# First tile's query products in another order, with VectorE's readings and a set of weight sums in other places

## The chip, the cores and the metric

The kernel runs on one core of a Trainium2 chip. A core has TensorE (matrix products, called PE in the profile), VectorE (DVE), ScalarE (ACT), GpSimd (POOL) and SyncE (SP), which issues most of the transfers here. Each engine works through its own list of instructions in the order in which they were written, and waits on semaphores for the others. The metric is the device time of one execution in microseconds (us); smaller is better.

## The reference

One layer of attention with many query heads and one shared key and value head, for 64 batches of 128 tokens with 512 features. Cut to what matters:

```python
xn = layernorm(x, g_in)                        # x: (64, 128, 512)
q = (xn @ Wq).reshape(b, n, 16, 64) * 64**-0.5 # Wq: (512, 1024)
k, v = split(xn @ Wkv)                         # Wkv: (512, 128)
k, v = [null_key; k], [null_value; v]          # null_kv: 2 rows of cond_64
sim = q @ k.T + [null_attn_bias; attn_bias]    # attn_bias: (16, 128, 128)
sim = -max where the key lies ahead of the query or is masked
out = softmax(sim) @ v                         # (64, 16, 128, 64)
out = out.reshape(b, n, 1024) @ Wo             # Wo: (1024, 512)
return x + layernorm(out, g_out)
```

All of it is float32.

## The kernel before

Four batches form a *group* (16 groups), two batches a *pair* (32 pairs). The main loop goes over pairs, `for d in range(1, 30): turn(d); body(d)`, and ends with two pairs of shorter work. While the softmax of pair d runs, a body also makes half of the queries, keys and values of the next group, and projects the output of pair d - 1 through Wo. So three pairs are in flight, and TensorE always has products of some stage to do. The order of every engine's work is the order of the calls in the source: there is no scheduler that changes it.

*`turn(d)`* makes the scores of the pair's two batches a and b, adds them to the bias (`scores_add`, VectorE), takes maxima, and multiplies the previous pair's weights by the values (`values`, L805). The sums with the bias free the PSUM tiles into which `values` then writes.

*`body(d)`* is what the change touches. With h = d % 2 it handles two tiles of queries, f0 = 2h and f1 = 2h + 1. Bodies with even d are called even, the others odd. A query tile is not made by eight products of blocks but by seven, with sums of blocks of weights (`wS`) and of tokens (`xS`, made by `token_sum` on GpSimd), as in Winograd's form of Strassen's method. `product(g, f, k, ...)` (L539) is product k, two matmuls of 128x256 in the source, four in the trace (the float32 passes are seen apart). They add up in two PSUM tiles:

- `pa` holds product 1; a copy `p1` (L551, ScalarE) is kept. Product 6 is added to it, and a copy `u2` is kept. Product 7 is added, and a copy `u3` is kept. Product 4 is added, and the tile is copied out (L557).
- `pc` holds product 5; with `u3` it gives one part of the result (`q_out`, L560, VectorE). Product 3 is added; with `u2` it gives another (L560 again). Only then may the next tile's product 5 take `pc`.

Each addition into `pa` must wait until ScalarE has made the copy before it; product 3 must wait for the first reading of `pc`.

Product 2 gives the last part. From d = 2 on (`deep`) it is itself made of seven small products for two tiles at once (`inner_product`, L605, tile `pl`), whose results are read by `inner_out` (L621, VectorE). Their weight sums are made once, by `weight_sums_inner` (L578, VectorE), in body 1, which still makes product 2 whole. Their token sums are made in each even body by `token_sums_inner` (L584, GpSimd).

The output projection is made in the same way: `out_sum` (L872, GpSimd), `out_product` (L892), copies `out_keep` (L906), readings `out_part` (L922, VectorE).

Around these a body carries: the exponentials (`exps`, L707, ScalarE), their reciprocal (`rinv`, L725, VectorE) and the scaling by it (`scale`, L729, GpSimd); `blocks_T` (L745, VectorE); the norm of a finished pair's output, namely `pair_norm` (L950, ScalarE), `pair_gain` (L953, VectorE), `pair_residual` (L956, VectorE) and the store; and the norm of the input of a later group, `norm_stats` (VectorE, with a power on GpSimd at L280), `norm_apply` (L301, ScalarE) and the transposes `tokens_T` (L325, VectorE). The last of these are done where `xw` is true, which it is not in the last two bodies (d = 28 and 29). `bias_add` (L641, GpSimd) lays out the bias of a later batch.

Of the kernel before, what the change touches and what calls it, by code (L numbers as in the profile page):

```python
# [17 lines left out]
def kernel(  # L18
# [66 lines left out]
    HC = NC // 2  # L85
# [423 lines left out]
    def token_sum(g, k):  # L509

        xS[g, k] = gp.tile([P, GB // 2, HK, N], FP, tag=f"xS{k}", name=f"xS{k}_{g}", bufs=1)
        lo, hi = xT[g][:, 0 : GB // 2], xT[g][:, GB // 2 :]
        b11, b12 = lo[:, :, lo_k], hi[:, :, lo_k]
        b21, b22 = lo[:, :, hi_k], hi[:, :, hi_k]
        p, m = {
            1: (b12, b11),
            2: (b22, xS.get((g, 1))),
            3: (b22, b12),
            4: (b21, xS.get((g, 2))),
        }[k]  # L520
        nc.gpsimd.tensor_tensor(xS[g, k], p, m, ALU.subtract)
# [58 lines left out]
    def token_sums_inner(g):  # L580

        x = gp.tile([P, 4, N], FP, tag="xL", name=f"xL_{g}", bufs=1)
        lo = xT[g][:, 0 : GB // 2]
        nc.gpsimd.tensor_tensor(x[:, 0:2], lo[:, 1, hi_k], lo[:, :, HK], ALU.subtract)  # L584
        nc.gpsimd.tensor_tensor(x[:, 2], lo[:, 1, KC - 1], x[:, 0], ALU.subtract)
        nc.gpsimd.tensor_tensor(x[:, 3], lo[:, 0, KC - 1], x[:, 2], ALU.subtract)
        xL[g] = x
# [114 lines left out]
    def exps(b, hf, lo=0, hi=R8):  # L702
        if hf == 0 and lo == 0:
            rsum[b] = small.tile([P, 2, R8], FP, tag="rsum", name=f"rsum_{b}")
        for k in range(lo, hi):
            row = S[b][:, k, WITH_NULL[hf]]
            nc.scalar.activation(  # L707
                row,
                row,
                AF.Exp,  # L710
                bias=nmax[b][:, hf, k : k + 1],
                accum_out=rsum[b][:, hf, k : k + 1],
            )
# [555 lines left out]
    def body(d):  # L1269

        a, b, p, l = 2 * d, 2 * d + 1, 2 * d - 2, 2 * d - 4
        g, h = d // 2 + 1, d % 2
        q, soft = g < NG, d > 0
        out, ln = 0 <= p <= P_LAST, 0 <= l <= P_LAST
        xw = g + 1 < NG
        m = (g + 1) * GB + 2 * h
        sums = q and h == 0 and d > 0
        f0, f1 = 2 * h, 2 * h + 1
        deep = q and d > 1

        if q:
            tags = [q_tags[g - 1, f, h] for f in range(NF)]
            q_tiles(g, (f0, f1), tags)
            pkv = kv_pair(g * GB + 2 * h)
        if soft:
            scores_max(b, 0)
            rinv(a, 0)
            scale(a, 0)
        if ln:
            pair_stats(l + 1)  # L1290
            pair_pow(l + 1)
        if sums:
            token_sums_inner(g)
        if q:
            kv_pair_out(g * GB + 2 * h, pkv)
            if h == 1:
                keys_T(g)
                values_spread(g)
        if h == 0 and g + 1 < NG:
            load_mask(g + 1)  # L1300
        if ln:
            pair_nmr(l)
            pair_nmr(l + 1)
        if xw:
            norm_stats(m)
            norm_stats(m + 1)
        if soft:
            scores_max(a, 1)
        if q:
            product(g, f0, 1, ps_q, "a")  # L1310
            keep("a", "p1")
        if ln:
            pair_norm(l)
        if deep:
            inner_product(g, h, 1)
            inner_out(g, h, 0, 0, 0, "p1")
        elif q:
            product(g, f0, 2, ps_w, "w")
            q_out(g, f0, 0, "w", "p1")
        if soft:  # L1320
            scores_max(b, 1)
        if xw:
            norm_nmr(m)
            norm_nmr(m + 1)
        if ln:
            pair_gain(l)
            pair_residual(l)
            store(l)
        if soft:
            exps(b, 0, 0, 4)  # L1330
        if sums:
            token_sum(g, 3)
        if out:
            out_sum(p, 0)
        if sums:
            token_sum(g, 4)
        if out:
            out_product(p, 1, ps_y, "X")
            out_keep("X", "yp1", "yp1")
            out_sum(p, 1)  # L1340
            out_sum(p, 2)
        if soft:
            exps(b, 0, 4, 6)
        if ln:
            pair_norm(l + 1, (ps_y, "Y"))
        if q:
            product(g, f0, 5, ps_q, "c")
            product(g, f0, 6, ps_q, "a", start=False)
            keep("a", "u2")
        if soft:  # L1350
            exps(b, 0, 6)
            rinv(b, 0)
        if out:
            out_product(p, 2, ps_w, "w")
            out_part(p, 0, "w", "yp1")
            out_sum(p, 3)
        if soft:
            scale(b, 0)
        if xw:
            norm_apply(m)  # L1360
        if q:
            product(g, f0, 7, ps_q, "a", start=False)
            keep("a", "u3")
        if deep:
            for k in (6, 5, 2):
                inner_product(g, h, k)
            inner_out(g, h, 0, 1, 0, "p1")
        if q:
            q_out(g, HC + f0, 1, "c", "u3")
        if deep:  # L1370
            inner_out(g, h, 0, 0, 2)
        if ln:
            pair_gain(l + 1)
            pair_residual(l + 1)
            store(l + 1)
        if xw:
            norm_apply(m + 1)
            tokens_T(m)
        if soft:
            exps(a, 1, 0, 1)  # L1380
        if q and not deep:
            product(g, f1, 2, ps_w, "w")
        if q:
            product(g, f0, 4, ps_q, "a", start=False)
            q_out(g, HC + f0, 0, "a")
            product(g, f0, 3, ps_q, "c", start=False)
            q_out(g, f0, 1, "c", "u2")
        if xw:
            tokens_T(m + 1)
            if h == 1:  # L1390
                tokens_out(g + 1)
                tokens_in(g + 1)
        if 0 <= p:
            for r in (p, p + 1):
                load_res(r)
        nm = m + 2
        if nm < B and xw:
            load_x(nm)
            load_x(nm + 1)
        if soft:  # L1400
            exps(a, 1, 1, 4)
        if q:
            product(g, f1, 1, ps_q, "a")
            keep("a", "p1")
        if deep:
            inner_product(g, h, 7)
            inner_out(g, h, 1, 1, 0, "p1")
            inner_out(g, h, 1, 1, 1)
        elif q:
            q_out(g, f1, 0, "w", "p1")  # L1410
        if soft:
            exps(a, 1, 4)
            rinv(a, 1)
            scale(a, 1)
            exps(b, 1, 0, 2)
        if q:
            product(g, f1, 5, ps_q, "c")
        if out:
            out_product(p, 5, ps_y, "Y")
            out_keep("Y", "yp5", "yp5")  # L1420
        if soft:
            exps(b, 1, 2, 3)
        if q:
            product(g, f1, 6, ps_q, "a", start=False)
            keep("a", "u2")
        if deep:
            inner_product(g, h, 4)
            inner_product(g, h, 3)
            inner_out(g, h, 1, 0, 0, "p1")
            inner_out(g, h, 0, 1, 1)  # L1430
        if soft:
            exps(b, 1, 3)
            blocks_T(a)
        if out:
            out_product(p, 6, ps_y, "X", start=False)
            out_keep("X", "yu2", "yu2")
        if soft:
            rinv(b, 1)
            scale(b, 1)
        if q:  # L1440
            product(g, f1, 7, ps_q, "a", start=False)
            keep("a", "u3")
            q_out(g, HC + f1, 1, "c", "u3")
        bias_add(b + 2)
        if d == PAIRS - 3:
            bias_add(B - 1)
        if out:
            out_product(p, 3, ps_y, "Y", start=False)
            out_part(p, 1, "Y", "yu2")
        if q:  # L1450
            product(g, f1, 3, ps_q, "c", start=False)
            q_out(g, f1, 1, "c", "u2")
        if out:
            pair_stats(p)
            pair_pow(p)
            out_product(p, 7, ps_y, "X", start=False)
            out_part(p + 1, 1, "X", "yp5")
        if soft:
            blocks_T(b)
        if q:  # L1460
            product(g, f1, 4, ps_q, "a", start=False)
            q_out(g, HC + f1, 0, "a")
        if out:
            out_product(p, 4, ps_y, "X", start=False)
            out_part(p + 1, 0, "X")
        if d == 1:
            weight_sums_inner()

    def gains_T():
        pg = ps_y.tile([P, KC], FP, tag="X", name="pg")  # L1470
# [177 lines left out]
```

## Time and profile before

| what | value |
|---|---|
| median of 3 runs | 1052.17 us (1051.85 to 1052.64) |
| profiled execution, its own time | 1051.84 us |
| its span, first to last instruction | 1050.0 us |
| granted TensorE clock, mean | 0.996 |
| TensorE busy | 1029.7 us (98%) |
| VectorE busy | 795.2 us (76%) |
| GpSimd busy | 745.5 us (71%) |
| ScalarE busy | 678.2 us (65%) |
| DMA, all queues | 105.13 MB, mean 100 GB/s |

The span leaves out what lies around the instructions, here 1.84 us. A row of the timeline reads: start in us, duration in us, engine, source line, operation, the tiles written and read, their shapes, how many instructions were merged, and in brackets the idle time before it and who ended it. A row of the waits reads: engine, its tile and line, for whom it waited, then microseconds in total, times, and the longest. A row of a window reads: stretch, its length, then for TensorE, its weight loads, VectorE, ScalarE and GpSimd the busy time and the number of instructions, then the granted clock, the DMA share and GB/s. Matmuls are pipelined, and their ends are modelled; so starts are compared with starts.

### The profile page before, as it was taken

What the parts mean: (1) busy time and instruction counts of PE and PEld (TensorE: products, weight loads), DVE (VectorE), ACT (ScalarE), POOL (GpSimd) and SP (SyncE); (2) the same over time, 40 slices, a digit from 0 to 9 for tenths busy, and PEclk for the clock granted to TensorE, in tenths of its full rate; (3) what the DMA queues carried; (4) which work ended last, traced back from release to release, by engine and by line L of the source; (5) the groups of instructions that cost most, each with busy time, mean ns of one, the idle gap of its engine ahead of it and who ended that gap; (6) DMA issues with size and microseconds to landing.
All of it is one profiled execution on the core that took longest, in us unless ns stands there. A gap on an engine that the chain in (4) does not pass through costs nothing.

```text
span 1050.0 us, 31371 instructions
## 1 busy us (share of the span) xinstructions
PE 1029.7 (98%) x12337; PEld 908.4 (87%) x12337; DVE 795.2 (76%) x1774; ACT 678.2 (65%) x2709; POOL 745.5 (71%) x579
## 2 busy tenths in 40 slices
PE   9998999999999999999999999999999999999997
PEld 8887888888888888888888888888888888888886
DVE  6867777777778777778777787777787777777697
ACT  4664676656776665776656866567766667756583
POOL 5996668677676766868577586776867668686676
PEclk9998999999999999999999999999999999999999
DMA  7513143151522415133151331515224151321311
GB/s 218 164 43 124 62 130 97 46 159 62 164 78 66 125 62 177 67 102 95 61 175 62 126 100 37 170 62 154 84 64 129 62 177 69 102 72 41 92 62 61
DMA packets 69227, 105.13 MB, mean 100 GB/s; under 512 B 9044, under 2 KB 33496, under 8 KB 67288
## 3 DMA queue, kind: packets, MB, share of 16 engines
q1 hardware_dynamic: 68784, 102.73, 31.1%
q8 instruction: 97, 1.59, 0.6%
q14 instruction: 50, 0.41, 0.1%
q10 hardware_dynamic: 296, 0.40, 0.1%
HBM read 67.45 MB, written 35.65 MB: 98 GB/s over the span
## 4 chain that ended last, share of the span: by engine, by line
PE 88%; DVE 9%; issue 1%; POOL 1%; DMA 0%; POOLq 0%; DVEq 0%
PE pyX L892 19%; PE pa L539 15%; PE pyY L892 10%; PE pc L539 8%; PE po L805 7%; PE pkv L353 6%; PE pyw L892 5%; PE pl L605 4%; PE pq L474 3%; PE ps L676 3%; PE sc_X L676 2%; DVE qT L560 2%; DVE y L956 2%; DVE yn L953 2%; DVE xb L325 2%; PE sc_Y L676 1%
## 5 line engine op out<-in xcount | busy, mean ns | idle before, releaser
L707 ACT ACTIVATE s<-s,nmax 128x65 f32<-128x65 f32 (+1 forms) x1024 | 372.2, 367 | 67.2 <-DVE nmax L698 67.2
L729 POOL TENSOR_TENSOR s<-s,rinv 128x512 f32<-128x512 f32 (+1 forms) x132 | 190.6, 1446 | 172.6 <-DVE rinv L725 172.6
L641 POOL TENSOR_TENSOR s<-biasp,mneg 128x1552 f32<-128x1552 f32 (+1 forms) x65 | 206.2, 3174 | 51.6 <-DVE s L691 38.2
L707 ACT ACTIVATION_READ_ACCUMULATOR s<-s,nmax 128x1 f32 x1024 | 194.7, 190 | 0.0
L539 PE MATMUL pa<-xS,wq 128*128 128x256 f32 x472 | 123.1, 383 | 0.0
L698 DVE TENSOR_REDUCE nmax<-s 128x8 f32<-128x1032 f32 (+1 forms) x128 | 121.5, 950 | 0.1
L557 ACT COPY qT<-pa 128x256 f32<-128x256 f32 x59 | 22.0, 372 | 144.3 <-PE pa L539 142.6
L745 DVE STREAM_TRANSPOSE sb<-s 128x1536 f32<-128x1536 f32 (+1 forms) x68 | 113.5, 1672 | 2.0 <-POOL s L729 2.0
L892 PE MATMUL pyX<-wo,oT 128*128 128x256 f32 x464 | 109.7, 379 | 0.0
L892 PE MATMUL pyX<-wT,oT 128*128 128x256 f32 x464 | 109.7, 379 | 0.0
L539 PEld LDWEIGHTS pa<-xS,wq 128*128 128x128 f32 x472 | 87.3, 190 | 11.5 <-issue 0.2
L892 PEld LDWEIGHTS pyX<-wo,oT 128*128 128x128 f32 x464 | 86.0, 190 | 10.5
L892 PEld LDWEIGHTS pyX<-wT,oT 128*128 128x128 f32 x464 | 85.9, 190 | 10.7
L621 DVE TENSOR_TENSOR qT<-pl,kp 128x128 f32<-128x128 f32 x112 | 31.3, 280 | 82.2 <-PE pl L605 80.9
L805 PE MATMUL po<-sb,vr 32*64 32x128 f32 (+1 forms) x3840 | 83.6, 316 | 4.7 <-DVE s L691 4.7
L805 PEld LDWEIGHTS po<-sb,vr 32*64 32x64 f32 x3840 | 72.9, 133 | 13.2 <-issue 10.4
L872 POOL TENSOR_TENSOR oT<-oT 128x512 f32<-128x512 f32 x64 | 80.4, 1275 | 3.0 <-PE pyw L892 0.8
L824 ACT ACTIVATE oT<-po,nv 128x512 f32<-128x512 f32 (+1 forms) x127 | 73.7, 654 | 1.5 <-POOL s L729 1.4
L551 ACT COPY ku<-pa 128x256 f32<-128x256 f32 x118 | 43.8, 371 | 45.8 <-PE pa L539 41.6
L280 POOL TENSOR_TENSOR rstd<-rstd,nhalf 128x1 f32<-128x1 f32 x64 | 35.5, 555 | 53.0 <-DVE rstd L279 50.7
L560 DVE TENSOR_TENSOR qT<-pc,ku 128x256 f32<-128x256 f32 x118 | 48.7, 413 | 30.6 <-ACT ku L551 16.7
L539 PE MATMUL pc<-xS,wS 128*128 128x256 f32 x236 | 63.3, 390 | 6.2 <-DVE qT L560 6.2
(185 smaller groups left out, 2406.6 us busy)
## 6 DMA issues: line engine op xcount, KB each, us to landing
res<-in_x_dram SPq DMA_DIRECT2D x64, 256.0 KB, 2.9
x<-in_x_dram SPq DMA_DIRECT2D x63, 256.0 KB, 4.4
out_dram<-y SPq DMA_DIRECT2D x63, 256.0 KB, 2.0
xd<-xb SPq DMA_DIRECT2D x14, 1024.0 KB
xT<-xd SPq DMA_DIRECT2D x56, 256.0 KB, 6.0
vr<-vd SPq DMA_DIRECT2D x64, 128.0 KB, 2.7
kT<-kd SPq DMA_DIRECT2D x64, 64.0 KB, 2.1
wo<-in_L_cond_Wo_dram SPq DMA_DIRECT2D x1, 2048.0 KB, 12.8
```

Source lines behind the costliest of these rows:

```text
L353: nc.tensor.matmul(pkv, xT[g][:, t, kc, :], wkv[:, kc, :], start=(kc == 0), stop=(kc == KC - 1),)
L539: nc.tensor.matmul(prod[tag], w[:, kc, f * P : (f + 1) * P], t[:, :, kc, :], start=(start and kc == 0), stop=(kc == HK - 1), skip_group_ch ...
L560: nc.vector.tensor_tensor(o, p, k, ALU.add)
L641: nc.gpsimd.tensor_tensor(S[b][:, :, keys], biasp[:, :, keys], mneg[:, t, keys] .unsqueeze(1) .broadcast_to([P, R8, keys.stop - keys.start ...
L698: nc.vector.tensor_reduce(nmax[b][:, hf], S[b][:, :, WITH_NULL[hf]], AX.X, ALU.max, negate=True)
L707: nc.scalar.activation(row, row, AF.Exp, bias=nmax[b][:, hf, k : k + 1], accum_out=rsum[b][:, hf, k : k + 1],)
L729: nc.gpsimd.tensor_tensor(sv, sv, rinvs[b, hf][:, lo:hi].unsqueeze(2).broadcast_to([P, hi - lo, sv.shape[2]]), ALU.mult,)
L745: nc.vector.transpose(sbs[b][:, :, lo:hi].rearrange("p j e q -> p e j q"), S[b][:, lo:hi, 1 : ROW - 1].rearrange("p e (j k) -> p e j k", k=Q),
L805: nc.tensor.matmul(po[s][rows, to : to + n], vr[g][quad, j, t, :], sb[quad, slots, r * NF : (r + 1) * NF, :], start=(turn == 0), stop=True ...
L824: nc.scalar.activation(to, src, AF.Identity, bias=nv2)
L872: eng.tensor_tensor(o, a, b, op)
L892: nc.tensor.matmul(prod[key], h[:, c, :], w[:, c, :], start=(start and c == 0), stop=(c == HC - 1), skip_group_check=not start,)
```

## The change

In `body(d)`, and there alone:

- Product 6 of the first tile is issued ahead of product 5, and its copy `u2` ahead of the second `pair_norm` on ScalarE.
- Product 7, its copy `u3` and the first reading of `pc` come ahead of the output's product 2; before, they came behind it, the reading behind the small products too. TensorE's order from the output's product 1 on was 5, 6, output 2, 7, small ones, 4, 3; it is now 6, 5, 7, output 2, small ones, 4, 3.
- The second `pair_gain` moves up with that reading, ahead of the reading of the output's product 2 (`out_part`).
- The first `tokens_T` moves behind the second reading of `pc`, so that both transposes follow it.
- The second `inner_out` of the first tile follows directly on the first one.
- `token_sum(g, 3)` on GpSimd (even bodies) moves up, directly behind `token_sums_inner`, and so ahead of the two powers of the input norm and of `out_sum(p, 0)`.
- `weight_sums_inner` (body 1 only) moves from the end of the body to behind the reading of the second tile's product 2.

```diff
         if sums:
             token_sums_inner(g)
+            token_sum(g, 3)
...
         if soft:
             exps(b, 0, 0, 4)
-        if sums:
-            token_sum(g, 3)
         if out:
             out_sum(p, 0)
...
         if soft:
             exps(b, 0, 4, 6)
+        if q:
+            product(g, f0, 6, ps_q, "a", start=False)
+            keep("a", "u2")
         if ln:
             pair_norm(l + 1, (ps_y, "Y"))
         if q:
             product(g, f0, 5, ps_q, "c")
-            product(g, f0, 6, ps_q, "a", start=False)
-            keep("a", "u2")
         if soft:
             exps(b, 0, 6)
             rinv(b, 0)
+        if q:
+            product(g, f0, 7, ps_q, "a", start=False)
+            keep("a", "u3")
+            q_out(g, HC + f0, 1, "c", "u3")
+        if ln:
+            pair_gain(l + 1)
         if out:
             out_product(p, 2, ps_w, "w")
             out_part(p, 0, "w", "yp1")
...
         if xw:
             norm_apply(m)
-        if q:
-            product(g, f0, 7, ps_q, "a", start=False)
-            keep("a", "u3")
         if deep:
             for k in (6, 5, 2):
                 inner_product(g, h, k)
             inner_out(g, h, 0, 1, 0, "p1")
-        if q:
-            q_out(g, HC + f0, 1, "c", "u3")
-        if deep:
             inner_out(g, h, 0, 0, 2)
+        elif q:
+            product(g, f1, 2, ps_w, "w")
         if ln:
-            pair_gain(l + 1)
             pair_residual(l + 1)
             store(l + 1)
         if xw:
             norm_apply(m + 1)
-            tokens_T(m)
         if soft:
             exps(a, 1, 0, 1)
-        if q and not deep:
-            product(g, f1, 2, ps_w, "w")
         if q:
             product(g, f0, 4, ps_q, "a", start=False)
             q_out(g, HC + f0, 0, "a")
             product(g, f0, 3, ps_q, "c", start=False)
             q_out(g, f0, 1, "c", "u2")
+        if xw:
+            tokens_T(m)
         if xw:
             tokens_T(m + 1)
...
         elif q:
             q_out(g, f1, 0, "w", "p1")
+            weight_sums_inner()
...
-        if d == 1:
-            weight_sums_inner()
```

## The prediction

> **What bounds the kernel now.** I read the granted clock first (0.996 on the one core), then the waits, then the chain that ended last, then the timeline of a turn, engine by engine. TensorE is nearly never idle, so only what holds it counts. Of the waits of TensorE's matmuls, the two longest are these:
>
> ```profile
> PE pc L539 <- DVE qT L560: 6.2, 26, 0.2
> PE po L805 <- DVE s L691: 4.7, 1, 4.7
> ```
>
> The first comes once in each of 26 bodies, the second once in the run. The next fence holds starts from narrow windows of the timeline (L353 opens a body, L676 a turn), and one stretch with its granted clock (0.50).
>
> ```profile
> 295.21 2.05 PE L353 MATMUL pkv<-wkv,xT 128*128 128x128 f32 x16
> 321.83 0.27 PE L676 MATMUL sc_Y<-kT,qT 64*64 64x64 f32 x2
> 327.14 2.05 PE L353 MATMUL pkv<-wkv,xT 128*128 128x128 f32 x16
> 933.71 2.05 PE L353 MATMUL pkv<-wkv,xT 128*128 128x128 f32 x16
> 965.13 1.60 PE L353 MATMUL pkv<-wkv,xT 128*128 128x128 f32 x12
> 91.54 0.27 PE L676 MATMUL sc_Y<-kT,qT 64*64 64x64 f32 x2
> 103.64 2.08 PE L353 MATMUL pkv<-wkv,xT 128*128 128x128 f32 x16
> 97.00:103.60 6.60, 4.46 (x120) 3.71 (x120) 6.52 (x14) 2.77 (x16) 1.27 (x2) 0.50 0.01 2
> ```
>
> An ordinary pair of batches takes 327.14 - 295.21 = 31.93 us. The pair from 933.71, whose body has no token transposes (xw is false), takes 31.42. From the start of a turn to its body it is 5.31 (321.83 to 327.14), but 12.10 at turn 2 (91.54 to 103.64): 6.8 us are lost there once, 4.7 of them in the wait above and the rest at half clock.
>
> TensorE in an odd body, from its first tile's product 5 on (two products; out 2; 7; the small ones; 4; 3; the next tile's 1; a small one; 5):
>
> ```profile
> 331.84 1.03 PE L539 MATMUL pc<-xS,wS 128*128 128x256 f32 x4
> 332.70 1.03 PE L539 MATMUL pa<-xS,wS 128*128 128x256 f32 x4
> 333.57 1.89 PE L892 MATMUL pyw<-wo,oT 128*128 128x256 f32 x8
> 335.30 1.03 PE L539 MATMUL pa<-xS,wq 128*128 128x256 f32 x4
> 336.16 0.61 PE L605 MATMUL pl<-xL,wL 128*128 128x128 f32 x4
> 336.60 0.39 PE L605 MATMUL pl<-xT,wq 128*128 128x128 f32 x2
> 336.83 1.09 PE L539 MATMUL pa<-xS,wq 128*128 128x256 f32 x4
> 337.75 1.08 PE L539 MATMUL pc<-xT,wS 128*128 128x256 f32 x4
> 338.67 1.03 PE L539 MATMUL pa<-xT,wq 128*128 128x256 f32 x4
> 339.53 0.38 PE L605 MATMUL pl<-xL,wq 128*128 128x128 f32 x2
> 340.16 1.13 PE L539 MATMUL pc<-xS,wS 128*128 128x256 f32 x4 [0.24 <-DVE qT L560]
> ```
>
> A product occupies 0.865 us (331.84 to 333.57 for two), an output product 1.73 (333.57 to 335.30), a small one 0.22 (336.60 to 336.83). So the last product was due at 339.75 and began at 340.16, 0.41 late; it also lasted 1.13 instead of 1.03, since its first weights were not loaded ahead. Together 0.51, which is also 31.93 - 31.42. VectorE shows why:
>
> ```profile
> 338.49 0.69 DVE L956 TENSOR_TENSOR y<-yn,res 128x512 f32<-128x512 f32 x1
> 339.09 0.70 DVE L325 STREAM_TRANSPOSE xb<-x 128x512 f32<-128x512 f32 x1
> 339.72 0.39 DVE L560 TENSOR_TENSOR qT<-pc,ku 128x256 f32<-128x256 f32 x1
> ```
>
> The reading of pc that frees it (339.72 to 340.11) stands behind gain, residual and a token transpose. TensorE follows 0.05 us behind its end.
>
> **The change part by part.** No instruction is added or removed; each queue keeps its work, so only waits change.
>
> (a) *Transposes behind the reading of pc, gain and the other reading ahead of out 2.* Between the small products and the reading only two short reads and the residual remain on VectorE. With the delay of (c), product 3 ends at 338.91 and the next product 5 is due at 339.99; VectorE is free by about 338.8, so it reads from about 339.1 to 339.5. The wait goes: 26 x 0.51 = -13.3 us. If the cover failed it would be this price again. The same bodies without transposes show no successor in the second tile: 31.42 is stable there. Both transposes follow the reading, up to about 340.8, and then the second tile's inner reads; the small product that waits for those comes only behind products 5 and 6 and an output product (3.46 us after 339.99).
>
> (b) *Product 7 ahead of out 2.* Its copy u3 and the reading of pc against u3 come earlier, so products 4 and 3 no longer wait for them. From 336.83 to 339.53 three products take 2.70 where 2.59 would do: 0.11 in each of 28 bodies (turns 2 to 29), -3.1 us.
>
> (c) *Product 6 ahead of 5, its copy u2 ahead of the second normalisation on ScalarE.* Product 7 adds to pa, which ScalarE must first have copied (u2). Before, out 2 lay between; now only product 5 (0.865) does. ScalarE, with "..." for the exponentials:
>
> ```profile
> 330.15 0.37 ACT L551 COPY kp<-pa 128x256 f32<-128x256 f32 x1 [0.44 <-PE pa L539]
> 330.42 0.79 ACT L950 ACTIVATE yn<-y,nmro,rstdo 128x512 f32<-128x512 f32 x1
> ...
> 332.46 0.35 ACT L906 COPY kyp<-pyX 128x256 f32<-128x256 f32 x1
> ...
> 333.39 0.77 ACT L950 ACTIVATE yn<-y,nmro,rstdo 128x512 f32<-128x512 f32 x1
> 334.10 0.37 ACT L551 COPY ku<-pa 128x256 f32<-128x256 f32 x1
> ```
>
> It waits for TensorE at kp only, and then works without a gap. The copy u2 takes the place of the normalisation: it starts at 333.39 whatever TensorE does, and ends at 333.76. Product 7 is due at 333.57. Add 0.05 for the release and 0.10 for weights not loaded ahead: 0.34 late, in odd bodies. In even bodies product 7 waits for two engines (GpSimd's third token sum too, long done), and the nearest row with two such waits, product 4 there, starts 0.15 behind the copy's end (304.80):
>
> ```profile
> 304.43 0.37 ACT L551 COPY ku<-pa 128x256 f32<-128x256 f32 x1 [0.52 <-PE pa L539]
> 304.95 1.10 PE L539 MATMUL pa<-xS,wq 128*128 128x256 f32 x4
> ```
>
> so 0.44. Sum 14 x 0.34 + 14 x 0.44 = +10.9 us. Bounds: 0.1 (the copy hidden, late by its release alone) and 0.6 (the old stall and some more) per body, 3 to 17 us; I take the worked value. The Trainium skill speaks against a part of it ("TensorE: Matmul & The Clock Gate", the table at its head): the engine's queue pulls weight loads ahead of matmuls in flight. By that rule the 0.10 falls away, 28 x 0.10 = 2.8 us less. The row at 340.16, 1.13 long behind a wait, says otherwise.
>
> (d) *Inner weight sums in turn 1, from its end into its middle.* At the end they held VectorE while the next turn's scores waited to be read, hence the 4.7 us:
>
> ```profile
> 91.09 0.38 DVE L578 TENSOR_TENSOR wL<-wq 128x256 f32<-128x256 f32 x1
> 91.51 3.35 DVE L578 TENSOR_TENSOR wL<-wL,wq 128x256 f32<-128x256 f32 x1
> 91.25 3.33 POOL L641 TENSOR_TENSOR s<-biasp,mneg 128x1552 f32<-128x1552 f32 x1 [0.48 <-DVE sb L745]
> ```
>
> The same operation takes 0.38 alone and 3.35 where it meets GpSimd's bias addition. The new place is behind the reading at 79.16:
>
> ```profile
> 79.16 0.42 DVE L560 TENSOR_TENSOR qT<-pw,kp 128x256 f32<-128x256 f32 x1 [0.28 <-ACT kp L551]
> 80.71 0.20 DVE L725 RECIPROCAL rinv<-rsum 128x8 f32<-128x8 f32 x1 [1.12 <-ACT s L707]
> 77.72 1.06 POOL L729 TENSOR_TENSOR s<-s,rinv 128x512 f32<-128x512 f32 x1
> 80.99 1.90 POOL L729 TENSOR_TENSOR s<-s,rinv 128x1024 f32<-128x1024 f32 x1 [2.20 <-DVE rinv L725]
> ```
>
> GpSimd is idle there from 78.78, and its next work waits for the reciprocal that now stands behind the sums. Both transposes (0.70 each) now come close ahead of it, so I let the reading move to about 79.5; the sums then run from 79.9 to some 81.4 (4 x 0.38). The reciprocal is 0.6 us late, and with it the scaling, a block transpose and the reading for the second product 3. Price 0 to 0.5, taken 0.2. Turn 2 becomes ordinary: -6.8 us.
>
> (e) *Third token sum earlier on GpSimd (even bodies).* It must come earlier since product 7 does. It passes the two powers of the input norms; VectorE uses these only behind the second maximum: nothing. Stores, loads and the token tiles' DMAs keep their order on SP; the last transpose of a body ends within 0.2 us of where it did: nothing.
>
> Sum: -13.3 - 3.1 + 10.9 - 6.8 + 0.2 = -12.1 us. The profiled execution took 1051.84, 0.33 under the median of the runs; from the median 1052.17 it gives 1040.1.
>
> **The rivals.** *u2 is hidden after all*: ScalarE comes to it sooner, and product 7 waits for nothing or its release alone. For it: product 6 ends 0.69 before the copy can start. Against: ScalarE has no gap from kp on. 1052.2 - 13.3 - 3.1 - 6.8 + 0.2 = 1029, up to 1032.
>
> *The weight sums meet GpSimd in the new place too.* The Trainium skill's "GPSIMD Engine Reference", section "Specifications", says that the two engines share their SBUF interfaces, with contention where a VectorE instruction has two SBUF inputs; the two rows at 91 agree. If they meet the scaling at 77.72 or a later operation, VectorE passes its lateness to turn 1's products and turn 2: up to the 6.8 stay, 1047. Against: the gap of 2.20 on GpSimd.
>
> *Slower.* ScalarE's queue is the one mechanism: where it comes to u2 later than its place in the old trace (its exponentials held by VectorE's maximum or the first normalisation), product 7 waits that much longer in 28 bodies. It decides from 0.43 us above my 0.39 mean, 0.82 per body (12.1 / 28 = 0.43). With 1.1 per body the time is 1060. Against: both inputs are there in the old trace, as ScalarE shows no wait.
>
> **How the numbers follow.** Forecast 0.72 (1036 to 1044), u2 hidden 0.14, sums that meet GpSimd 0.07, slower 0.05, unchanged 0.02. The range 1030 to 1047 leaves out the slower, unchanged and a part of the second case. 0.2% is about what a measurement of this kernel can tell from no change. Faster 0.92, within 0.2% 0.03, slower 0.05.
>
> **What would show it.** The waits should lose the row of 26 and the 4.7, and gain one of pa (L539) for ScalarE's ku (L551), about 28 times 0.1 to 0.2. Pairs should take 31.6 to 31.8 us throughout, those at the end longer than before (31.42). Turn 2 should reach its body in 5.3 us with the clock at 1.00. The L578 rows should be 0.4 us each near 80. I am wrong if product 7 shows no wait, if pc still waits for VectorE, or if a wait appears in the second tile.

## The result, and the profile after

The changed kernel took 1039.77 us (median of 4 runs, 1039.46 to 1039.88), the kernel before 1052.41 (4 runs): a ratio of 0.988, 95% interval 0.9863 to 0.9897. The prediction was 1040.1. Since a right sum can hide wrong terms, the profile and the runs below take it apart.

The profiled execution has a span of 1037.9 us, 12.1 less than before. Starts of turns and bodies say where:

| stretch | before | after | difference |
|---|---|---|---|
| start to turn 1 | 59.97 | 60.49 | +0.5 |
| turn 1 to turn 2 | 31.57 | 31.57 | 0.0 |
| turn 2 to turn 3 | 38.74 | 31.70 | -7.0 |
| turns 3 to 27 (25 pairs) | 798.12 | 792.02 | -6.1 |
| turns 28 and 29 | 62.85 | 63.34 | +0.5 |
| the rest | 58.8 | 58.8 | 0.0 |

The first row is work that the change does not touch; it differs between executions by this much. The third row holds two things: the loss that was special to turn 2, and the 0.23 by which ordinary pairs became shorter (31.93 to 31.70).

The longest waits of TensorE's matmuls, after, and one row of its weight loads (PEld); both long waits of before are gone, and one is new:

```profile
PE pa L539 <- ACT ku L551: 2.6, 15, 0.4
PE py_s L892 <- DVE oT L822: 1.4, 2, 0.8
PEld pa L539 <- ACT ku L551: 6.9, 14, 0.8
```

(Line numbers are those of the kernel before up to L1290, so the tiles' lines are unchanged.) The prediction expected the first row about 28 times and not 15. Those 15 are the 14 even bodies and the odd one of turn 19; the 14 waits of the weight loads are the odd bodies. The view of the matmuls lists the idle time of TensorE's array, whose modelled ends hide a part; starts show more. Rows of after's timeline, TensorE with one weight load, from windows at turn 2, an even body, an odd body (from its products 6, 5 and 7 on) and the two last bodies:

```profile
92.06 0.27 PE L676 MATMUL sc_Y<-kT,qT 64*64 64x64 f32 x2
97.37 2.05 PE L353 MATMUL pkv<-wkv,xT 128*128 128x128 f32 x16
...
292.95 1.03 PE L539 MATMUL pc<-xS,wS 128*128 128x256 f32 x4
294.14 1.10 PE L539 MATMUL pa<-xS,wq 128*128 128x256 f32 x4 [0.16 <-ACT ku L551]
...
323.79 1.03 PE L539 MATMUL pa<-xS,wS 128*128 128x256 f32 x4
324.65 1.03 PE L539 MATMUL pc<-xS,wS 128*128 128x256 f32 x4
325.75 0.73 PEld L539 LDWEIGHTS pa<-xS,wq 128*128 128x128 f32 x4 [0.47 <-ACT ku L551]
325.75 1.13 PE L539 MATMUL pa<-xS,wq 128*128 128x256 f32 x4
326.72 1.89 PE L892 MATMUL pyw<-wo,oT 128*128 128x256 f32 x8
...
329.11 1.03 PE L539 MATMUL pa<-xS,wq 128*128 128x256 f32 x4
331.70 0.38 PE L605 MATMUL pl<-xL,wq 128*128 128x128 f32 x2
331.93 1.03 PE L539 MATMUL pc<-xS,wS 128*128 128x256 f32 x4
...
921.09 2.05 PE L353 MATMUL pkv<-wkv,xT 128*128 128x128 f32 x16
952.79 2.05 PE L353 MATMUL pkv<-wkv,xT 128*128 128x128 f32 x16
```

Turn 2 reaches its body in 5.31 us. The next tile's product 5 (331.93) follows its neighbour without delay. Product 7 was due 0.865 behind product 5's start, at 325.515 in the odd body and 293.815 in the even one; it began 0.235 and 0.325 late and lasted 0.10 and 0.07 too long. So it costs 0.34 and 0.40. The pair from 921.09, which had 31.42 before, now takes 31.70, like all others.

ScalarE (exponentials left out) and VectorE in the same odd body:

```profile
324.41 0.35 ACT L906 COPY kyp<-pyX 128x256 f32<-128x256 f32 x1
...
325.34 0.35 ACT L551 COPY ku<-pa 128x256 f32<-128x256 f32 x1
325.60 0.78 ACT L950 ACTIVATE yn<-y,nmro,rstdo 128x512 f32<-128x512 f32 x1
```

```profile
329.98 0.68 DVE L956 TENSOR_TENSOR y<-yn,res 128x512 f32<-128x512 f32 x1
331.04 0.42 DVE L560 TENSOR_TENSOR qT<-pc,ku 128x256 f32<-128x256 f32 x1 [0.38 <-PE pc L539]
331.38 1.29 DVE L325 STREAM_TRANSPOSE xb<-x 128x512 f32<-128x512 f32 x2
```

The copy u2 starts at 325.34, although product 6 was issued by 324.65: it is ScalarE that is late. VectorE now waits for TensorE before the reading of pc, and no longer the other way round. The stretch from 97.00 to 103.60 has the clock at 1.00 (0.50 before):

```profile
97.00:103.60 6.60, 6.60 (x68) 5.92 (x52) 5.79 (x18) 6.17 (x23) 6.13 (x10) 1.00 0.01 2
```

One pair alone falls out: that of turn 19 takes 31.92 instead of 31.64. There the copy u2 came 0.28 later against the products than elsewhere, and ScalarE was that late already at the copy p1 ahead of it. The fifth, sixth and seventh run below show the same at the same pair; what delays it is not shown.

### The profile page after: what moved, and what is told of

Its sections match the earlier page's. It is cut to its first block, busy times and chain, and to the rows that moved or that the text cites. A ratio compares the mean times of both kernels' runs of the same rounds, so it can differ in the third digit from the quotient of the medians.

```text
span 1037.9 us, 31399 instructions
## 1 busy us (share of the span) xinstructions
PE 1024.5 (99%) x12337; PEld 903.0 (87%) x12337; DVE 788.7 (76%) x1774; ACT 675.7 (65%) x2709; POOL 745.1 (72%) x579
## 4 chain that ended last, share of the span: by engine, by line
PE 85%; ACT 6%; DVE 6%; issue 1%; POOL 1%; DMA 0%; POOLq 0%; DVEq 0%; ACTq 0%
PE pa L539 17%; PE pyX L892 15%; PE pyY L892 10%; PE pc L539 7%; PE po L805 7%; PE pkv L353 6%; PE pyw L892 5%; PE pl L605 4%; ACT s L707 3%; PE ps L676 3%; PE pq L474 3%; PE sc_X L676 2%; DVE st L269 2%; DVE nmax L698 2%; PE sc_Y L676 2%; PE py_s L892 1%
## 5 line engine op out<-in xcount | busy, mean ns | idle before, releaser
L539 PEld LDWEIGHTS pa<-xS,wq 128*128 128x128 f32 x472 | 85.1, 190 | 23.9 <-POOL rstd L280 7.0
L892 PEld LDWEIGHTS pyX<-wT,oT 128*128 128x128 f32 x464 | 85.9, 190 | 10.7
L805 PE MATMUL po<-sb,vr 32*64 32x128 f32 (+1 forms) x3840 | 81.5, 310 | 0.0
L353 PE MATMUL pkv<-wkv,xT 128*128 128x128 f32 x512 | 65.2, 281 | 0.0
L353 PEld LDWEIGHTS pkv<-wkv,xT 128*128 128x128 f32 x512 | 59.6, 191 | 5.0 <-DVE s L691 4.8
```

What stands on the lines that cost most here:

```text
L353: nc.tensor.matmul(pkv, xT[g][:, t, kc, :], wkv[:, kc, :], start=(kc == 0), stop=(kc == KC - 1),)
L539: nc.tensor.matmul(prod[tag], w[:, kc, f * P : (f + 1) * P], t[:, :, kc, :], start=(start and kc == 0), stop=(kc == HK - 1), skip_group_ch ...
L805: nc.tensor.matmul(po[s][rows, to : to + n], vr[g][quad, j, t, :], sb[quad, slots, r * NF : (r + 1) * NF, :], start=(turn == 0), stop=True ...
L892: nc.tensor.matmul(prod[key], h[:, c, :], w[:, c, :], start=(start and c == 0), stop=(c == HC - 1), skip_group_check=not start,)
```

## The experiments

My theory is the prediction's: four separate terms, each a wait with one owner. The rivals are that the terms depend on each other (so that the sum was right by luck), that product 7 is late for another reason than ScalarE's place in its queue, and that VectorE's lateness had other causes than the transpose. Ratios are to the kernel before, timed on the same chip. That kernel's median lay between 1051.84 and 1052.41 us in these comparisons, so differences in us between two runs are good to some 0.6.

**The weight sums alone.** The kernel before, with one edit:

```diff
             q_out(g, f1, 0, "w", "p1")
+            weight_sums_inner()
...
-        if d == 1:
-            weight_sums_inner()
```

> The kernel before with one edit: the inner weight sums of body 1 in their new place, all else as before. My theory: the whole loss at turn 2 goes and nothing else. Turn 2 took 38.74 us before and 31.70 after, so 7.0 us less than 1052.4: 1045.4; the granted clock is 1.00 around 100 us, the four sums take 0.4 us each, and the 26 waits of pc for VectorE stay. Rival (the sums meet GpSimd's work in any place and only shift the wait): 1050 to 1052.

Measured 1045.60 us, ratio 0.9939 (0.9924 to 0.9954). The old wait stays to the last digit, and turn 2 takes 31.93, 6.8 less than before:

```profile
PE pc L539 <- DVE qT L560: 6.2, 26, 0.2
```

So this term stands by itself. The expected 7.0 was too much, since it held the 0.23 of the shorter ordinary pair, which this run does not have. The time fell by 6.2 and not by 6.8: in its profile body 1 starts at 66.00, in that of before at 65.38, and that lies ahead of the edit (the eleven profiles of this document differ there by up to 0.6).

**Sums and transposes, products in the old order.** The kernel before with the edit above and:

```diff
             norm_apply(m + 1)
-            tokens_T(m)
...
         if xw:
+            tokens_T(m)
             tokens_T(m + 1)
```

> The kernel before with two edits: the weight sums as in the first run, and both token transposes behind the second reading of pc; the products stay in their old order (5, 6, output 2, 7). My theory: the place of the transpose alone made the old wait of 0.51 us in 26 bodies, and the new order of the products only brought the wait for u2. Then 1045.4 - 13.3 = 1032.1, some 7.5 us under the changed kernel, with pairs of 31.42 us. Rival (the old wait came from VectorE's gain and first reading as well, so that the readings must come ahead of output 2): part of the wait stays, 1035 to 1040.

Measured 1032.59, ratio 0.9816 (0.9801 to 0.983), pairs of 31.42 throughout. Against the run before it, 13.0 us: this one move removes the whole old wait. VectorE then reads pc directly behind the residual:

```profile
328.51 0.69 DVE L956 TENSOR_TENSOR y<-yn,res 128x512 f32<-128x512 f32 x1
329.12 0.41 DVE L560 TENSOR_TENSOR qT<-pc,ku 128x256 f32<-128x256 f32 x1
```

It is also 7.2 us faster than the changed kernel, which has the same two moves and the rest of the change besides. So that rest, as the change has it, costs more than it gives; the next run shows which part.

**The copy u2 ahead of two exponentials.** The changed kernel with

```diff
-        if soft:
-            exps(b, 0, 4, 6)
         if q:
             product(g, f0, 6, ps_q, "a", start=False)
             keep("a", "u2")
+        if soft:
+            exps(b, 0, 4, 6)
```

> The changed kernel with product 6 and its copy u2 ahead of the exponentials 4 and 5 on ScalarE, not behind them. My theory: product 7 waits for u2 only because ScalarE reaches the copy late. The copy then starts when product 6 has ended, some 0.45 us sooner, and ends before product 5 does: the waits of pa for ku go, 28 bodies x (0.34 or 0.40) = 10.3 us, 1039.8 - 10.3 = 1029.5, pairs of 31.3 us. Rival A (product 7 is late for another reason, as the first weights after a change of tile): no change, 1039.8. Rival B (the exponentials, put off, make the next copy or the scaling late): 1032 to 1038 with a new wait for ku at product 4.

Measured 1029.09, ratio 0.9783 (0.9766 to 0.9799), pairs of 31.30. TensorE and ScalarE in an odd body of this run:

```profile
321.18 1.03 PE L539 MATMUL pa<-xS,wS 128*128 128x256 f32 x4
322.05 1.03 PE L539 MATMUL pc<-xS,wS 128*128 128x256 f32 x4
322.91 1.03 PE L539 MATMUL pa<-xS,wq 128*128 128x256 f32 x4
```

```profile
321.81 0.35 ACT L906 COPY kyp<-pyX 128x256 f32<-128x256 f32 x1
322.30 0.37 ACT L551 COPY ku<-pa 128x256 f32<-128x256 f32 x1
```

The copy now ends at 322.67, before product 5 gives way, and product 7 starts without delay. 10.7 us came from moving one copy past two exponentials on an engine that is busy two thirds of the time. This is the best of all runs, 1.0% faster than the changed kernel.

**The copy u2 later still.** The changed kernel with

```diff
             product(g, f0, 6, ps_q, "a", start=False)
-            keep("a", "u2")
         if ln:
             pair_norm(l + 1, (ps_y, "Y"))
+        if q:
+            keep("a", "u2")
```

> The changed kernel with the copy u2 behind the second normalisation on ScalarE, which is its order before the change, while product 6 stays ahead of product 5. The normalisation takes 0.71 us from start to start. My theory: product 7 waits that much longer in 28 bodies, +19.9 us, 1039.8 + 19.9 = 1059.7, slower than the kernel before; the waits of pa for ku grow by 0.7 each. Rival (the copy is not what product 7 waits for): 1039.8.

Measured 1059.37, ratio 1.007 (1.005 to 1.009): slower than the kernel before. Pairs take 32.36 and 32.42 us, 0.72 more each. The waits:

```profile
PE pa L539 <- ACT ku L551: 11.9, 15, 0.9
PE pa L539 <- POOL yS L872: 11.4, 13, 0.9
```

In even bodies product 7 waits for two engines, and the view names GpSimd for 13 of them. But ScalarE held both kinds: the copy starts 0.70 later behind product 5 in all 28 bodies, both kinds of pairs grew by 0.72, and product 7 still begins 0.05 (odd) or 0.14 to 0.15 (even) behind the copy's end. Between this run and the one before it, the copy's place alone moves the time by 30 us.

**The weight sums back at the end.** The changed kernel, with the last hunk of its diff undone:

```diff
             q_out(g, f1, 0, "w", "p1")
-            weight_sums_inner()
...
+        if d == 1:
+            weight_sums_inner()
```

> The changed kernel with the inner weight sums back at the end of body 1. My theory: the loss at turn 2 comes back by itself, 7.0 us, 1046.8, with the wait of po for VectorE (4.7 us) and the clock at half for some 7 us from about 97 us on. Rival (the rest of the change would have hidden it, since VectorE's order is another): 1040 to 1043.

Measured 1046.36, ratio 0.9946 (0.9929 to 0.9962); turn 2 takes 38.49 us, 6.8 more than in the changed kernel, with the clock at 0.50 for 6.8 us from 96.95 on. So the rest of the change does not hide it. The old wait of po is back:

```profile
PE po L805 <- DVE s L691: 4.7, 1, 4.7
```

**The weight sums where GpSimd is busy.** The changed kernel with them some 6 us later in body 1 than the change puts them:

```diff
             q_out(g, HC + f1, 1, "c", "u3")
+        if d == 1:
+            weight_sums_inner()
         bias_add(b + 2)
```

> The changed kernel with the inner weight sums some 5 us later in body 1, where GpSimd is in its second scaling (1.9 us) and then in the bias addition (3.2 us). My theory: a VectorE operation with two operands in SBUF waits until the GpSimd operation that it meets has ended. The first of the four then lasts about 1.8 us, the second about 3.2, the others 0.4; VectorE is free some 4.5 us late, the readings of the output's parts come late and TensorE waits 3 to 5 us before its last output product of body 1: 1043 to 1046. Rival (the lengths at the old place came from something else, as the scores of turn 2): four of 0.42, at most 1 us in all, 1040 to 1041.

Measured 1044.15, ratio 0.9923 (0.9903 to 0.9943), from two executions 1.6 us apart; the profile is of the longer one. The four sums, what GpSimd did then, and where TensorE waited:

```profile
L578 DVE TENSOR_TENSOR wL<-wq x1: 1842/1842/1842, 85.8 to 85.8; 128x256 f32<-128x256 f32 x1
L578 DVE TENSOR_TENSOR wL<-wL,wq x1: 3305/3305/3305, 87.7 to 87.7; 128x256 f32<-128x256 f32 x1
L578 DVE TENSOR_TENSOR wL<-wq,wL x1: 425/425/425, 91.1 to 91.1; 128x256 f32<-128x256 f32 x1
L578 DVE TENSOR_TENSOR wq<-wq x1: 417/417/417, 91.4 to 91.4; 128x256 f32<-128x256 f32 x1
```

```profile
85.50 1.91 POOL L729 TENSOR_TENSOR s<-s,rinv 128x1024 f32<-128x1024 f32 x1 [2.31 <-DVE rinv L725]
87.36 3.38 POOL L641 TENSOR_TENSOR s<-biasp,mneg 128x1552 f32<-128x1552 f32 x1
```

```profile
PE pyX L892 <- DVE y L922: 3.7, 1, 3.7
```

Each of the first two lasts until just behind the end of its neighbour on GpSimd (87.68 behind 87.41, 91.03 behind 90.74). The same operation takes 0.42 where GpSimd is idle. The Trainium skill's "GPSIMD Engine Reference", section "Specifications", states this contention for VectorE instructions with two SBUF inputs; these rows agree. In them each sum ended 0.27 to 0.29 us behind the GpSimd operation that it met, whether that one had 1.6 or 3.0 us left to run.

**The first transpose back ahead of the reading.** The changed kernel with

```diff
             norm_apply(m + 1)
+            tokens_T(m)
...
-        if xw:
-            tokens_T(m)
```

> The changed kernel with the first token transpose back ahead of the second reading of pc. In the profile of the changed kernel VectorE has 0.38 us to spare before that reading, and the reading ends some 0.25 us before TensorE needs it; a transpose holds VectorE 0.63. Theory A (the reading is then about 0.25 late, just in time for the weights): no change beyond 1 us, 1039.8 to 1040.8, so either of the two moves alone would have been enough beside product 7's wait. Theory B (the transpose's place is the one cause of the old wait): the 0.5 us in 26 bodies come back, 1052 or 1053.

Measured 1039.55, ratio 0.988 (0.9865 to 0.9895): no difference to the changed kernel. Theory A holds. Two cures of the old wait stand side by side in the change: the transposes behind the reading, and the gain and first reading ahead of output 2. Here the second was enough without the first; in the second run the first was enough without the second.

**The same with product 7 in time.** The third run's kernel with the edit just shown.

> The third run's kernel (copy u2 early, 1029.1 us) with the first token transpose back ahead of the second reading of pc. Product 7 is no longer late there, so TensorE needs pc 0.34 us sooner behind an unchanged VectorE. From that run's rows: in an odd body VectorE ends the residual at 328.0, the transpose would end at 328.64 and the reading at 329.03, where product 5 is due at 328.98; with the release and unloaded weights it is 0.2 late. In an even body (residual to 296.23, reading to 297.26, product due at 297.68) it is in time. Theory: 13 odd bodies x 0.2 = 2.6 us, 1031.7, odd pairs 31.5, even pairs 31.3. Rival (the transpose no longer matters at all): 1029.1.

Measured 1030.98, ratio 0.98 (0.9783 to 0.9816), 1.9 more than the third run; odd pairs 31.46, even pairs 31.30. An odd body, TensorE and VectorE:

```profile
329.08 0.38 PE L605 MATMUL pl<-xL,wq 128*128 128x128 f32 x2
329.36 1.13 PE L539 MATMUL pc<-xS,wS 128*128 128x256 f32 x4
```

```profile
328.29 0.70 DVE L325 STREAM_TRANSPOSE xb<-x 128x512 f32<-128x512 f32 x1
328.92 0.39 DVE L560 TENSOR_TENSOR qT<-pc,ku 128x256 f32<-128x256 f32 x1
```

Once TensorE comes 0.34 sooner, the second cure alone is 0.06 + 0.10 us short in odd bodies, where 0.2 was expected.

**The third token sum back.** The third run's kernel with

```diff
             token_sums_inner(g)
-            token_sum(g, 3)
...
             exps(b, 0, 0, 4)
+        if sums:
+            token_sum(g, 3)
```

> The third run's kernel with the third token sum back behind the exponentials' first part, so behind the two powers on GpSimd. In the kernel before it ran from 300.57 to 301.84 in an even body, where product 7 is now due at 301.64. Theory (it had to come earlier): product 7 waits for GpSimd in 14 even bodies, about 0.28 + 0.10 late, 5.3 us, 1034.4, with a wait of pa for xS (L521). Rival (it would have been in time): 1029.1.

Measured 1033.67, ratio 0.9825 (0.9811 to 0.984), 4.6 more. The wait of TensorE's weight loads, then TensorE and GpSimd in an even body:

```profile
PEld pa L539 <- POOL xS L521: 6.4, 13, 0.5
```

```profile
291.93 1.03 PE L539 MATMUL pc<-xS,wS 128*128 128x256 f32 x4
293.05 1.13 PE L539 MATMUL pa<-xS,wq 128*128 128x256 f32 x4
```

```profile
291.72 1.27 POOL L521 TENSOR_TENSOR xS<-xT 128x512 f32<-128x512 f32 x1
```

The sum ends at 292.99, and product 7, due at 292.79, begins 0.06 behind it. That is 0.36 in 13 even bodies, not in the 14 expected: in the last one, without the input's norm, GpSimd has no powers to do there and is in time.

## Why the prediction was right

Point by point, in the prediction's letters.

(a) *The old wait of pc.* -13.3 us foretold; 13.0 measured where it was taken away by itself (first and second run). The mechanism was right. The text called two moves one step; they are two cures. The transposes' move suffices alone in the old order of products (second run). The other suffices alone while product 7 is late (seventh run), and no longer in odd bodies once it is in time (eighth run).

(b) *Products 4 and 3 no longer late.* 0.11 per pair foretold, 3.1 us. In the changed kernel product 4, product 3 and the next product 1 take 2.59 (329.11 to 331.70), as worked out; the second run, in the old order, still has the 0.11, and its pairs take 31.42 against 31.30 in the third.

(c) *The new wait for u2.* +10.9 foretold: 0.34 in odd and 0.44 in even bodies. The profile shows 0.34 and 0.40, 10.4 in all and 10.6 with the 0.28 of turn 19; taking the wait away gave 10.7, and lengthening it by 0.71 gave +19.6 where 19.9 follows. The even term was 0.04 too large: the start lay 0.14 behind the copy's end, as its row had said (0.15), but the product then lasted 1.10, not 1.13, so it lost 0.07 to weights not loaded ahead and not 0.10. The Trainium skill ("TensorE: Matmul & The Clock Gate", the table at its head) has weight loads pulled ahead of matmuls in flight. The trace agrees where nothing is waited for: output 2's load begins at 326.50, 0.22 ahead of its product. But the load of product 7 did not pass its wait. It begins at 325.75, together with the product, so the 0.10 (0.07 in even bodies) did not fall away.

(d) *The weight sums.* -6.8 foretold at turn 2. The first run measured 6.8 there by starts and the fifth 6.8 the other way; their times moved by 6.2 and 6.6, since the start of the program differs between executions. For body 1 the prediction took +0.2; from the start of body 1 to turn 2 it is 26.16 in both profiles, so nothing. The sums ran from 80.2 to 81.9. Everything from body 1 on is 0.5 later in this profile, so by the clock of the old one they ran from 79.7 to 81.4, where 79.9 to 81.4 was worked out; they took 0.42 each instead of 0.38. That they would not meet GpSimd was right. The sixth run gives the price at a place where they do: 4.4 us by the times, 5.5 in the profiled execution from body 1 to turn 2. The prediction had allowed up to 6.8.

(e) *The third token sum.* That it must come earlier was right: without its move product 7 is late again in 13 bodies, once u2 is not (ninth run). That the move itself costs nothing was not tried alone; no wait in the changed kernel speaks against it.

The sum fell 0.3 from the median, the profiled execution's own sum (-12.1) on the mark; in part by luck: (c) was 0.3 too large and the price in body 1 0.2, and 0.5 of the span came from work ahead of turn 1 that the change does not touch, which happens to make up for both. Two of the rivals were made real: "u2 is hidden" gives 1029.1 where 1029 was worked out, and "slower" gives 1059.4 for 1.1 us per body where 1060 was.

## What to carry to other kernels

Where the bounding engine waits for a copy, ask at which place of its queue the copying engine reaches it, not how busy that engine is: here two exponentials of 0.34 us each ahead of one copy cost 10.7 us of 1040. Reordering the bounding engine's own work can remove the cover behind which other engines made such copies, so each move needs the question what now lies between the write and the next write. And where a change has several moves against one wait, try each alone; here the smaller change (sums and transposes) was 0.7% faster than the whole.

## What the runs showed of the hardware

Apart from the first and the last microseconds of each run, the records have TensorE at half clock for 6.8 us in the kernel before (from 96.89) and in the fifth run (from 96.95), and for 3.4 us, half as long, in the sixth (from 93.70). The matmuls' wait was 4.7 us in the first two and 3.7 in the sixth. The stretch before the fall in the kernel before, then the sixth run:

```profile
93.48:96.89 3.41, 0.97 (x36) 0.73 (x28) 3.38 (x3) 0.00 (x0) 3.33 (x3) 1.00 0.16 59
```

```profile
90.00:93.70 3.70, 0.18 (x1) 0.00 (x0) 3.60 (x9) 0.37 (x1) 0.87 (x2) 1.00 0.49 179
93.70:97.10 3.40, 3.22 (x8) 2.52 (x8) 1.81 (x2) 0.00 (x0) 1.93 (x2) 0.50 0.22 81
```

So a wait of 3.7 us cost body 1 of the sixth run 5.5 us (31.70 from its start to turn 2 instead of 26.16). The Trainium skill ("TensorE: Matmul & The Clock Gate", "What's actually happening") gives an idle window of about 3.4 us, free-running, after which the clock is halved. The 3.4 and 6.8 us at half clock agree with one and two such windows, and so does the fall in the sixth run, 3.5 us into its wait. In the kernel before, the clock fell only 2.4 us into the wait, at the end of 3.4 us in which TensorE had been busy for 0.97; so a window idle from end to end was not needed there. The 28 waits of the fourth run, of 0.9 us at most, left the clock at 1.00.
